# A graph network's node update: one product moved to the dealing stage, and the edge counts laid on all partitions

## The chip, the cores and the metric

The kernel runs on one core of one Trainium2 chip. The metric is device time in microseconds, the median over the timed runs. A profiled execution, which is a run of its own, gives the trace. Engines: PE (TensorE), DVE (VectorE), ACT (ScalarE), POOL (GpSimd), SP (SyncE, which only issues transfers here).

## The reference, cut to what matters

Four layers follow one another over a graph of 3125 nodes (256 features each) and 53125 edges: a message-passing layer, a mixture of experts, a mean-aggregation layer and an MLP over chosen tokens. The change touches the first:

```python
msg_input  = concatenate([node[i], node[j], edge_attr])        # 256 + 256 + 16
h          = relu(msg_input @ mW1 + mb1)                       # 512 hidden units, per edge
messages   = h @ mW2 + mb2                                     # 256
aggregated = segment_sum(messages, i)                          # over the edges of node i
u          = relu(concatenate([node, aggregated]) @ uW1 + ub1) # 512
x          = node + u @ uW2 + ub2
```

`node` is the layer-normalized input. The sum over edges is linear, so the kernel sums `h` per node first and multiplies by `mW2` once per node; `mb2` then comes in times the number of the node's edges, `deg`. All is float32 at the ends; some products work with rounded halves.

## The kernel before, in words

The nodes lie in 25 blocks of 128 (`NB`), the edges in 416 tiles of 128, taken as 104 chunks of four tiles.

**Dealing** (`deal`). The loop over chunks `c` sorts the edges into buckets of 32 source nodes. For each chunk, `buckets` makes one-hots on DVE, `select` ranks the edges by products on PE, `place` works out each edge's row on DVE and builds the edge's record `rt` (with a copy by ACT), and `put` has POOL store the four tiles with one indirect transfer each into `cbuf`. `rt` and its row number `to` have rings of 20 buffers. For the first 13 chunks, `halve_attributes` also turns the edge attributes on PE. The order on PE, DVE, ACT and SP is the one written; POOL runs free and works off its stores.

Into the same loop is woven the generator `tables`, which goes through the 25 node blocks. For each block it normalizes the rows (DVE), turns them (PE, L133, into `xTa`), makes the two node products of the message layer (`pp`, L314 and L316), copies and splits them (ACT, DVE) and stores five tiles through SP: `tab_b`, `tab_a`, two halves in `tab_h`, and the turned rows in `xT0`. It yields four times a block, and the loop takes one step from it in each chunk from `c >= 3` on: 101 steps for 100 yields. At `c == 2` the loop splits the attribute weights `w_ea` (L420, L421), which SP has loaded after the first eight node blocks and `mw1`. After the loop, a check of the counts writes `fits`, on which all engines branch.

**Buckets** (`edges_by_bucket`). 125 steps: 25 units of four buckets, five rounds each. A step makes the source side by PE (`spread`, `pa`), adds the gathered target side `cb` on DVE, takes the relu on ACT (`relu`), and sums the hidden units by source on PE (`by_source`, `ph`). POOL gathers `cb` from `tab_b` three steps ahead (L712). Two generators fill the gaps: `tally` (`counts`: one-hots `oa`, `ob` on DVE, products `pn` on PE, copies `cn` on ACT, stored by SP) and `nodes_left` (`finish_nodes` for the last pair of node blocks: `update`, normalization, `experts`, normalization, `sends`). A step takes up to four slots of the first and three of the second. At the end of a unit `close` copies the summed hidden units into `hsb` and puts the edge counts into its last column.

`update` works on a pair of blocks. It loads the pair's turned rows (`xT0g`), turns the sums (L529) and the counts (`pdeg`, L532, one row), multiplies by `mW2` with the counts times `mb2` as a last product over one partition (`pagg`, L539, L541), copies to `aT` (L542), makes four output groups of `uW1` with `dense` (L514 on PE: two products with `xT0g`, two with `aT`; then relu with bias on ACT, L515), and multiplies by `uW2` (`pupd`, L554, added to `x` on DVE at L556). Three PSUM banks are shared in turn by all small products of this stage.

After the buckets come the mean-aggregation layer (`sums_of_few`, `padj`) and the MLP, which the change does not touch.

Of the kernel before, what the change touches and what calls it, by code (L numbers as in the profile page):

```python
# [11 lines left out]
I32 = mybir.dt.int32  # L12
# [38 lines left out]
def gnn_ffn_kernel(ctx: ExitStack, tc: tile.TileContext, a: dict, out: bass.AP):  # L51
# [103 lines left out]
    xT0 = dram.tile([P, 2, NP], F32, name="xT0")  # L155
# [21 lines left out]
    def deal():  # L177
# [46 lines left out]
        for k in range(0, NB - 1, 8):  # L224
            nc.sync.dma_start(x[:, k:k + 8, :], a["x"][k * P:(k + 8) * P].rearrange("(k p) d -> p k d", p=P))
            if k == 0:
# [5 lines left out]
                nc.vector.memset(one_row, 1.0)  # L232
                w_ea = tp.tile([32, HID], F32, name="w_ea", bufs=1)
# [69 lines left out]
        def tables():  # L303
            for k in range(NB):
                xns = layernorm_rows(k, 1, True, nc.vector)
                yield
                xT = tp.tile([P, 2, P], F32, name="xTa")
# [22 lines left out]
                nc.sync.dma_start(xT0[:, :, rows], xT)  # L330
# [3 lines left out]
        with tc.tile_pool(name="deal", bufs=3) as dp:  # L334
# [34 lines left out]
            def place(c, out):  # L369
# [10 lines left out]
                to, f = dp.tile([P, GB], I32, name="to", bufs=20), dp.tile([P, GB], F32, name="f")  # L380
# [5 lines left out]
                rt = dp.tile([P, GB, RW], F32, name="rt", bufs=20)  # L386
# [19 lines left out]
            for c in range(-1, chunks):  # L406
# [17 lines left out]
                if c >= 3:  # L424
                    next(making, None)
# [35 lines left out]
    def rest_of(fast):  # L461
# [17 lines left out]
        mb2 = load(wl0, "mb2", [1, D], a["L0_gnn_mb2"].rearrange("(o m) -> o m", o=1))  # L479
        uw1 = weight(wl0, "uw1", a["L0_gnn_uW1"])  # L480
        ub1 = col_bias(wl0, "ub1", a["L0_gnn_ub1"], HID)
# [37 lines left out]
        def update(k0, nb, sums):  # L519
            n = nb * P  # L520
            xT = st["up"].tile([P, 2, UB * P], F32, name="xT0g")
            nc.sync.dma_start(xT[:, :, :n], xT0[:, :, k0 * P:k0 * P + n])
            hT = st["up"].tile([P, 4, UB * P], F32, name="hT", bufs=1)
            deg = st["up"].tile([1, UB * P], F32, name="deg", bufs=1)
            for i in range(nb):
                h0 = sums[i]
# [4 lines left out]
                pg = bank("pdeg")  # L531
                nc.tensor.matmul(pg[:1, :P], lhsT=h0[:, HID:HW], rhs=ident, start=True, stop=True)  # L532
                nc.vector.tensor_copy(deg[:, i * P:(i + 1) * P], pg[:1, :P])
                yield
            aT = st["up"].tile([P, 2, UB * P], F32, name="aT", bufs=1)
            for m in range(2):
                pd = bank("pagg")
                for c in range(4):
                    nc.tensor.matmul(pd[:, :n], lhsT=mw2[:, c, m * P:(m + 1) * P], rhs=hT[:, c, :n],  # L539
                                     start=c == 0, stop=False)  # L540
                nc.tensor.matmul(pd[:, :n], lhsT=mb2[:, m * P:(m + 1) * P], rhs=deg[:, :n], start=False, stop=True)  # L541
                nc.vector.tensor_copy(aT[:, m, :n], pd[:, :n])  # L542
                yield
            uT = st["up"].tile([P, 4, UB * P], F32, name="uT", bufs=1)
            ins = [xT[:, c, :n] for c in range(2)] + [aT[:, c, :n] for c in range(2)]
            for m in range(4):
                dense(uT[:, m, :n], [uw1[:, c, m * P:(m + 1) * P] for c in range(4)], ins, n, ub1[:, m:m + 1])
# [836 lines left out]
```

## Time and profile before

| | |
|---|---|
| median of 3 timed runs | 2482.83 us (2481.05 to 2484.32) |
| profiled execution | 2345.68 us, of which span 2343.4 us |
| mean granted PE clock in it | 0.863 |
| busy: PE, DVE, ACT, POOL | 1863.8, 1452.8, 952.0, 985.8 us |
| POOL's stores of dealt edges (L396) | 416, 992 ns each |
| POOL's gathers (L712) | 490, 978 ns each |
| `pp` on PE while edges are dealt (L314) | 200, 852 ns each |
| transfers, over the span | 309.76 MB, mean 132 GB/s |

A row of a window or of a group gives an engine's busy time in it, and the number of its instructions in parentheses. PE's matmuls are pipelined and overlap in the records, so a row of eight that spans 1.7 us costs 0.22 us each, whatever the mean of one says. A line of the waits reads: engine and line that waited, `<-` what ended the wait, the total in us, how often, and the longest.

### The profile page before, as it was taken

The numbers are of one execution on the slowest core, as the hardware profiler recorded it, in microseconds if no ns is written. First come the engines' busy times: TensorE is split into PE (matmuls) and PEld (weight loads), VectorE is DVE, ScalarE is ACT, GpSimd is POOL, SyncE is SP. The second block draws the span as 40 slices with busy tenths as digits, with TensorE's granted clock in tenths as the row PEclk, the third lists the DMA queues.
The fourth block names the chain that finished last, engine by engine and source line by source line (L and its number), as shares of the span: only waits on it lengthen the run. The fifth ranks groups of instructions, "written<-read, shape, count | busy, mean of one in ns | idle before, by whom it ended". The sixth has DMA issues, their size and how long they took to land. (4 is left out here: it accounts for less than half of the span.)

```text
span 2343.4 us, 26626 instructions
## 1 busy us (share of the span) xinstructions
PE 1863.8 (80%) x8262; PEld 1121.3 (48%) x8262; DVE 1452.8 (62%) x3985; ACT 952.0 (41%) x1682; POOL 985.8 (42%) x1032
## 2 busy tenths in 40 slices
PE   3787787820488988888988988988868999998598
PEld 1333333310154554554554544544535777885366
DVE  5777777730376666666666666666536765668921
ACT  1222222200366655655655655655423333442111
POOL 3777777776564544544554554454100000110000
PEclk9767676755698988998998998999978999999799
DMA  9223223221975655655655655664125456540010
GB/s 276 88 88 104 91 91 105 88 68 45 304 226 151 194 160 153 199 175 149 196 176 155 190 174 163 185 174 135 48 79 158 114 130 157 127 112 1 0 37 21
DMA packets 234590, 309.76 MB, mean 132 GB/s; under 512 B 34313, under 2 KB 165236, under 8 KB 234070
## 3 DMA queue, kind: packets, MB, share of 16 engines
q1 hardware_dynamic: 178358, 157.62, 22.7%
q0 software_dynamic: 52512, 142.96, 21.1%
q10 hardware_dynamic: 3568, 7.38, 0.9%
q8 instruction: 68, 1.11, 0.2%
q14 instruction: 84, 0.69, 0.1%
HBM read 226.18 MB, written 81.69 MB: 131 GB/s over the span
## 5 line engine op out<-in xcount | busy, mean ns | idle before, releaser
L712 POOL DMA_INDIRECT cb<-tab_b,goes_to x490 | 479.4, 978 | 533.7 <-issue 239.6
L396 POOL DMA_INDIRECT cbuf<-rt,to x416 | 412.6, 992 | 162.9 <-issue 99.3
L750 DVE TENSOR_TENSOR cb<-pa,cb 128x1024 f32<-128x1024 f32 x245 | 288.8, 1217 | 181.5 <-PE pa L745 152.2
L1279 PE MATMUL padj<-z,slab 128*128 128x512 f32 x1250 | 320.0, 409 | 15.7 <-DVE z L1188 15.4
L755 ACT ACTIVATE cb<-cb 128x1024 f32<-128x1024 f32 x245 | 257.7, 1052 | 101.8 <-DVE cb L750 98.7
L1279 PEld LDWEIGHTS padj<-z,slab 128*128 128x128 f32 x1250 | 232.3, 191 | 74.7 <-issue 24.0
L745 PE MATMUL pa<-gives,oT 128*128 128x512 f32 x490 | 175.6, 486 | 36.2 <-ACT oT L107 31.6
L107 ACT ACTIVATE oT<-pt 64x512 fp32r<-64x512 f32 (+1 forms) x250 | 144.5, 578 | 132.9 <-PE pt L731 129.1
L802 PE MATMUL pn<-ob,oa 128*128 128x448 f16 (+1 forms) x692 | 160.5, 351 | 21.1 <-DVE ob L787 8.3
L125 POOL TENSOR_TENSOR x<-x,xn 128x256 f32<-128x256 f32 x25 | 24.5, 978 | 351.5 <-DVE xn L122 351.5
L783 DVE TENSOR_SCALAR oa<-ids,rows 128x128 f16<-128x128 f16 x692 | 163.1, 262 | 0.0
L787 DVE TENSOR_SCALAR ob<-ids,rows 128x448 f16<-128x448 f16 (+1 forms) x490 | 161.6, 330 | 0.0
L133 PE MATMUL pt<-ident,xn 128*128 128x128 f32 x200 | 52.5, 361 | 128.1 <-DVE xn L122 64.3
L314 PE MATMUL pp<-mw,xTa 128*128 128x512 f32 x200 | 142.7, 852 | 0.0
L761 PE MATMUL ph<-cb,rows 128*32 128x512 f32 x980 | 140.4, 623 | 0.0
L745 PEld LDWEIGHTS pa<-gives,oT 128*128 128x128 f32 x490 | 102.6, 221 | 69.5 <-ACT oT L107 43.5
L107 ACT ACTIVATE cn<-pn 128x352 f16<-128x352 f32 x196 | 98.0, 500 | 93.2 <-PE pn L802 74.1
L731 PE MATMUL pt<-ident_r,rows 128*64 128x128 f32 x490 | 56.8, 238 | 91.1 <-DVE goes_to L705 91.1
L731 PEld LDWEIGHTS pt<-ident_r,rows 128*64 128x64 f32 x490 | 39.7, 139 | 178.6 <-issue 139.5
L514 PE MATMUL pd<-xT,fw 128*128 128x512 f32 (+1 forms) x224 | 92.7, 570 | 34.2 <-DVE y L1330 34.2
L1206 ACT ACTIVATE slab<-two 128x2048 fp32r<-128x2048 f16 x50 | 95.6, 1911 | 41.1 <-PE padj L1279 38.8
L117 ACT ACTIVATE rstd<-mv,eps 128x1 f32<-128x1 f32 (+1 forms) x76 | 22.4, 295 | 220.7 <-DVE mv L115 220.7
(224 smaller groups left out, 3163.7 us busy)
## 6 DMA issues: line engine op xcount, KB each, us to landing
two<-adj_h SPq DMA_DIRECT2D x24, 1600.0 KB, 8.1
rows<-cbuf SPq DMA_DIRECT2D x25, 680.0 KB, 8.5
gives<-tab_h SPq DMA_DIRECT2D x48, 256.0 KB, 8.8
adj_h<-cn SPq DMA_DIRECT2D x100, 112.0 KB, 2.5
adj_h<-cn SPq DMA_DIRECT2D x100, 88.0 KB, 3.2
cb<-tab_b,goes_to POOLq DMA_INDIRECT x490, 4.1
cbuf<-rt,to POOLq DMA_INDIRECT x416, 2.2
cbuf<-empty ACTq DMA_DIRECT2D x4, 1632.0 KB
```

The lines of the kernel that those rows point to most:

```text
L107: nc.scalar.activation(dst, src, AF.Copy)
L314: nc.tensor.matmul(pp, lhsT=xT[:, c, :], rhs=mw1[:, 2 * h + c, :], start=c == 0, stop=h == 1 and c == 1)
L396: one_of = nc.gpsimd.indirect_dma_start(out=cbuf[:], out_offset=bass.IndirectOffsetOnAxis(ap=to[:n, i:i + 1], axis=0), in_=rt[:n, i, :], i ...
L712: nc.gpsimd.indirect_dma_start(out=cb[:, j, :], out_offset=None, in_=tab_b[:], in_offset=bass.IndirectOffsetOnAxis(ap=u["to"][:, i:i + 1], ...
L745: nc.tensor.matmul(got[j // 2][:, j % 2, :], lhsT=oT[:, j, :], rhs=u["ag"][:, j, :], start=True, stop=True)
L750: nc.vector.tensor_tensor(cb[:, j:j + 2], pa, cb[:, j:j + 2], op=OP.add)
L755: nc.scalar.activation(h, h, AF.Relu)
L761: nc.tensor.matmul(u["ph"][j * BN:(j + 1) * BN, :], lhsT=u["rows"][:, GB * r + j, :BN].bitcast(F32), rhs=hs[j // 2][:, j % 2, :], start=r ...
L783: nc.vector.tensor_scalar(oa, ids[:, 1 + i * P:1 + (i + 1) * P], field[:, 0:1], None, op0=OP.is_equal)
L787: nc.vector.tensor_scalar(ob[:, :w], ids[:, 1:w + 1], field[:, 1:2], None, op0=OP.is_equal)
L802: nc.tensor.matmul(pn[:, :w], lhsT=u["oa"].pop((j, r, i)), rhs=u["ob"][j, r][:, :w], start=r == rs[0], stop=r == rs[-1])
L1279: nc.tensor.matmul(pa, lhsT=slab[:, c, :], rhs=(z2 if second else z1)[:, c, :], start=c == 0, stop=c == NB - 1)
```

## The change

The product of the normalized rows with the upper half of `uW1` moves from `update` into `tables`. `tables` now keeps the turned rows of two blocks in one tile; after the second it makes four groups of 128 outputs (two products each, over 256 columns), ACT adds the bias `ub1` and writes `ut`, and one store puts it in `own` (DRAM, 512 outputs by node), in place of the stores of `xT0`. `uw1a` and `ub1` are therefore loaded in `deal`, ahead of `w_ea`. `tables` yields 14 times a pair, 177 times in all, and the loop takes one step in even chunks and two in odd ones. The rings of `rt` and `to` go from 20 to 12.

`update` loads `ux` from `own` instead of `xT0g`; it makes only the two products with `aT`, adds `ux` on DVE, and takes the relu on ACT for two groups at a time. The edge counts come from `close` on all 128 partitions (the one-hot sums multiplied by ones), so the turns of `pdeg` and the one-partition products go, and `aT` is made by one DVE operation for each block: counts times `mb2`, now a value per partition, plus `pd`. The path through `hsum` (`deg is None`), which runs only if the edges don't fit, makes the counts in `update`.

```diff
--- before.py
+++ after.py
@@ -152,7 +152,7 @@
     zres = dram.tile([NP, 2 * D], F32, name="zres")
 
 
-    xT0 = dram.tile([P, 2, NP], F32, name="xT0")
+    own = dram.tile([P, 4, NP], F32, name="own")
 
     first = ExitStack()
     ring(first)
@@ -230,6 +230,9 @@
                 nc.sync.dma_start(mb1, a["L0_gnn_mb1"].rearrange("(o m) -> o m", o=1))
                 one_row = tp.tile([1, P], F32, name="one_row", bufs=1)
                 nc.vector.memset(one_row, 1.0)
+                uw1a = tp.tile([P, 2, HID], F32, name="uw1a", bufs=1)
+                nc.sync.dma_start(uw1a, a["L0_gnn_uW1"][:D].rearrange("(k p) m -> p k m", p=P))
+                ub1 = col_bias(tp, "ub1", a["L0_gnn_ub1"], HID)
                 w_ea = tp.tile([32, HID], F32, name="w_ea", bufs=1)
                 for i in range(2):
                     nc.sync.dma_start(w_ea[16 * i:16 * (i + 1)], a["L0_gnn_mW1"][2 * D:2 * D + 16])
@@ -301,10 +304,14 @@
 
 
         def tables():
+            pair = []
             for k in range(NB):
                 xns = layernorm_rows(k, 1, True, nc.vector)
                 yield
-                xT = tp.tile([P, 2, P], F32, name="xTa")
+                if not pair:
+                    two = tp.tile([P, 2, UB * P], F32, name="xTa")
+                pair.append(two)
+                xT = two[:, :, (len(pair) - 1) * P:len(pair) * P]
                 layernorm_turn(xns, xT)
                 yield
                 ts = []
@@ -327,7 +334,19 @@
                 nc.sync.dma_start(tab_a[rows, :], ts[0])
                 nc.sync.dma_start(tab_h[rows, 0, :], first.bitcast(F32))
                 nc.sync.dma_start(tab_h[rows, 1, :], rest.bitcast(F32))
-                nc.sync.dma_start(xT0[:, :, rows], xT)
+                yield
+                if k % UB == UB - 1 or k == NB - 1:
+                    n = len(pair) * P
+                    ut = tp.tile([P, 4, UB * P], F32, name="ut", bufs=1)
+                    for m in range(4):
+                        pu = bank("pu")
+                        for c in range(2):
+                            nc.tensor.matmul(pu[:, :n], lhsT=uw1a[:, c, m * P:(m + 1) * P], rhs=pair[0][:, c, :n],
+                                             start=c == 0, stop=c == 1)
+                        nc.scalar.activation(ut[:, m, :n], pu[:, :n], AF.Identity, bias=ub1[:, m:m + 1])
+                        yield
+                    nc.sync.dma_start(own[:, :, (k + 1) * P - n:(k + 1) * P], ut[:, :, :n])
+                    pair.clear()
                 yield
 
 
@@ -377,13 +396,13 @@
                 rnd = dp.tile([P, GB], I32, name="rnd")
                 nc.vector.tensor_scalar(rnd, rank, P.bit_length() - 1, None, op0=OP.logical_shift_right)
 
-                to, f = dp.tile([P, GB], I32, name="to", bufs=20), dp.tile([P, GB], F32, name="f")
+                to, f = dp.tile([P, GB], I32, name="to", bufs=12), dp.tile([P, GB], F32, name="f")
                 nc.vector.scalar_tensor_tensor(f, rnd, float(GB - P * PER), base[:, at], op0=OP.mult, op1=OP.add)
                 nc.vector.scalar_tensor_tensor(f, rank, float(PER), f, op0=OP.mult, op1=OP.add)
                 nc.vector.scalar_tensor_tensor(f, rank, float(CAP), f, op0=OP.is_lt, op1=OP.mult)
                 nc.vector.tensor_tensor(to, f, past[:, at], op=OP.add)
                 pos[c] = to
-                rt = dp.tile([P, GB, RW], F32, name="rt", bufs=20)
+                rt = dp.tile([P, GB, RW], F32, name="rt", bufs=12)
                 nc.vector.tensor_tensor(rt[:, :, :BN], nodes.unsqueeze(1).to_broadcast([P, GB, BN]),
                                         row[:, at, AT_SRC - BN:AT_SRC - BN + 1].to_broadcast([P, GB, BN]), op=OP.is_equal)
                 copy(rt[:, :, BN:], row[:, at, :])
@@ -422,7 +441,8 @@
                     nc.sync.dma_start(w_h[:, 0, :], wf.bitcast(F32))
                     nc.sync.dma_start(w_h[:, 1, :], wr.bitcast(F32))
                 if c >= 3:
-                    next(making, None)
+                    for _ in range(1 + c % 2):
+                        next(making, None)
                 if c + 2 < chunks:
                     ohs.pop(c, None)
 
@@ -476,9 +496,8 @@
             queue[0] = Held
 
         mw2 = weight(wl0, "mw2", a["L0_gnn_mW2"])
-        mb2 = load(wl0, "mb2", [1, D], a["L0_gnn_mb2"].rearrange("(o m) -> o m", o=1))
-        uw1 = weight(wl0, "uw1", a["L0_gnn_uW1"])
-        ub1 = col_bias(wl0, "ub1", a["L0_gnn_ub1"], HID)
+        mb2 = col_bias(wl0, "mb2", a["L0_gnn_mb2"], D)
+        uw1 = weight(wl0, "uw1", a["L0_gnn_uW1"][D:])
         uw2 = weight(wl0, "uw2", a["L0_gnn_uW2"])
         ub2 = row_bias(wl0, "ub2", a["L0_gnn_ub2"], D)
         sw1 = weight(wl0, "sw1", a["L0_ffn_sW1"])
@@ -518,33 +537,43 @@
 
         def update(k0, nb, sums):
             n = nb * P
-            xT = st["up"].tile([P, 2, UB * P], F32, name="xT0g")
-            nc.sync.dma_start(xT[:, :, :n], xT0[:, :, k0 * P:k0 * P + n])
+            ux = st["up"].tile([P, 4, UB * P], F32, name="ux")
+            nc.sync.dma_start(ux[:, :, :n], own[:, :, k0 * P:k0 * P + n])
             hT = st["up"].tile([P, 4, UB * P], F32, name="hT", bufs=1)
-            deg = st["up"].tile([1, UB * P], F32, name="deg", bufs=1)
+            degs = []
             for i in range(nb):
-                h0 = sums[i]
+                h0, deg = sums[i]
                 pt = bank("pt4")
                 for c in range(4):
                     nc.tensor.transpose(pt[:, c * P:(c + 1) * P], h0[:, c * P:(c + 1) * P], ident)
                 copy(hT[:, :, i * P:(i + 1) * P], pt.rearrange("p (c n) -> p c n", c=4))
-                pg = bank("pdeg")
-                nc.tensor.matmul(pg[:1, :P], lhsT=h0[:, HID:HW], rhs=ident, start=True, stop=True)
-                nc.vector.tensor_copy(deg[:, i * P:(i + 1) * P], pg[:1, :P])
+                if deg is None:
+
+                    deg = st["up"].tile([P, P], F32, name="deg")
+                    pg = bank("pdeg")
+                    nc.tensor.matmul(pg[:, :P], lhsT=h0[:, HID:HW].to_broadcast([P, P]), rhs=ident, start=True, stop=True)
+                    nc.vector.tensor_copy(deg, pg[:, :P])
+                degs.append(deg)
                 yield
             aT = st["up"].tile([P, 2, UB * P], F32, name="aT", bufs=1)
             for m in range(2):
                 pd = bank("pagg")
                 for c in range(4):
                     nc.tensor.matmul(pd[:, :n], lhsT=mw2[:, c, m * P:(m + 1) * P], rhs=hT[:, c, :n],
-                                     start=c == 0, stop=False)
-                nc.tensor.matmul(pd[:, :n], lhsT=mb2[:, m * P:(m + 1) * P], rhs=deg[:, :n], start=False, stop=True)
-                nc.vector.tensor_copy(aT[:, m, :n], pd[:, :n])
+                                     start=c == 0, stop=c == 3)
+                for i in range(nb):
+                    nodes_of = slice(i * P, (i + 1) * P)
+                    nc.vector.scalar_tensor_tensor(aT[:, m, nodes_of], degs[i], mb2[:, m:m + 1], pd[:, nodes_of],
+                                                   op0=OP.mult, op1=OP.add)
                 yield
             uT = st["up"].tile([P, 4, UB * P], F32, name="uT", bufs=1)
-            ins = [xT[:, c, :n] for c in range(2)] + [aT[:, c, :n] for c in range(2)]
             for m in range(4):
-                dense(uT[:, m, :n], [uw1[:, c, m * P:(m + 1) * P] for c in range(4)], ins, n, ub1[:, m:m + 1])
+                pd = bank("pd")
+                for c in range(2):
+                    nc.tensor.matmul(pd[:, :n], lhsT=uw1[:, c, m * P:(m + 1) * P], rhs=aT[:, c, :n], start=c == 0, stop=c == 1)
+                nc.vector.tensor_tensor(uT[:, m, :n], pd[:, :n], ux[:, m, :n], op=OP.add)
+                if m % 2:
+                    nc.scalar.activation(uT[:, m - 1:m + 1, :n], uT[:, m - 1:m + 1, :n], AF.Relu)
                 yield
             for i in range(nb):
                 k = k0 + i
@@ -763,14 +792,17 @@
 
                 def close(u):
                     m = u["m"]
-                    hs = bp.tile([P, HW], F32, name="hsb", bufs=3)
-                    copy(hs[:m, :HID], u["ph"][:m])
+                    hs = bp.tile([P, HID], F32, name="hsb", bufs=3)
+                    copy(hs[:m], u["ph"][:m])
+                    deg = bp.tile([P, P], F32, name="degs", bufs=3)
                     pt = bank("pt")
-                    nc.tensor.matmul(pt[:m, :1], lhsT=u["oss"].rearrange("p j s -> p (j s)")[:, :m], rhs=one, start=True, stop=True)
-                    copy(hs[:m, HID:HW], pt[:m, :1])
+                    nc.tensor.matmul(pt[:, :m], lhsT=one.to_broadcast([P, P]), rhs=u["oss"].rearrange("p j s -> p (j s)")[:, :m],
+                                     start=True, stop=True)
+                    copy(deg[:, :m], pt[:, :m])
                     if m < P:
                         nc.vector.memset(hs[m:], 0.0)
-                    return hs
+                        nc.vector.memset(deg[:, m:], 0.0)
+                    return hs, deg
 
                 def one_hots(u, j, rs):
 
@@ -1055,7 +1087,7 @@
                     for k in range(k0, k0 + nb):
                         hs = st["up"].tile([P, HW], F32, name="h0")
                         nc.sync.dma_start(hs, hsum[k * P:(k + 1) * P, :])
-                        got.append(hs)
+                        got.append((hs, None))
                     for _ in finish_nodes((k0, nb), got):
                         pass
             rings.pop()
```

## The prediction, made before the change was run

> **What bounds the kernel now.** I read the page's slices first, then a table of windows, then the steps of one pair of node blocks, then the waits.
>
> The 40 slices show three stages: dealing the edges until slice 10, the buckets with the node update until slice 29, then the last convolution and the MLP. One wide window for each of the first two, and one for the tail of the first (columns: window, its length, busy us and count for each engine, granted clock, DMA share, GB/s):
>
> ```profile
> 60.00:480.00 420.00, 330.09 (x1286) 141.02 (x1285) 309.80 (x1026) 107.64 (x323) 319.71 (x322) 0.71 0.29 95
> 490.00:580.00 90.00, 0.19 (x2) 0.11 (x2) 3.06 (x9) 0.00 (x0) 67.50 (x71) 0.50 0.10 31
> 640.00:1640.00 1000.00, 863.53 (x4263) 515.23 (x4262) 667.24 (x1915) 595.05 (x1002) 503.02 (x532) 0.92 0.59 175
> ```
>
> From 490 to 580 us PE, DVE and ACT stand idle and POOL alone works off indirect stores: the dealing stage ends with POOL, whose last store ends at 578.8 us. Its pace is 90 us over 71 stores, 1.27 us each, 5.1 us for a chunk of four. The other engines deal 98 chunks in 420 us, 4.3 us each, so they end 90 us early. In the buckets PE is busy 86% at a clock of 0.92. What waits confirms it: SP, which would load the first bucket, sits behind those stores, and in the bucket stage others wait for PE:
>
> ```profile
> SPq L695 <- DMA cbuf<-rt,to: 85.4, 5, 80.8
> ACT uT L515 <- PE pd L514: 65.8, 33, 2.8
> DVE aT L542 <- PE pagg L541: 29.0, 11, 2.7
> PE pdeg L532 <- ACT oT L107: 14.2, 10, 1.4
> ```
>
> Then one pair of node blocks, cut at the starts of four bucket steps; `update` runs in them:
>
> ```profile
> 1026.20:1032.00 5.80, 4.39 (x33) 2.56 (x32) 4.48 (x13) 4.73 (x7) 4.51 (x5) 1.00 0.77 220
> 1032.00:1042.65 10.65, 10.40 (x53) 6.71 (x52) 7.35 (x27) 5.02 (x9) 5.13 (x7) 1.00 0.94 297
> 1042.65:1051.35 8.70, 8.70 (x49) 6.31 (x48) 5.90 (x15) 5.35 (x10) 4.60 (x6) 1.00 0.50 143
> 1051.35:1059.15 7.80, 7.80 (x45) 5.12 (x44) 4.84 (x12) 4.86 (x8) 1.98 (x3) 1.00 0.37 114
> ```
>
> PE fills the second to fourth window (10.40 of 10.65, 8.70 of 8.70, 7.80 of 7.80). The update's matmuls set these steps' length, so what is taken from PE here shortens them until DVE (7.35, 5.90) is full.
>
> **The change part by part.** Sums are against the profiled execution, 2345.68 us (span 2343.4). The median of the timed runs, 2482.83, lies 137 us or 5.8% above it; nothing here says where those are spent, so I scale the difference by 1.058.
>
> *Taken from the bucket stage, per full pair (12 of them).* The product with the nodes' own features is 16 matmul instructions. Back to back the chain has eight of `pd L514` in 1.73 us, so 0.216 each: 3.5 us. The two bias products (`pagg<-deg,mb`, L541) hold PE from 1034.86 to 1035.48: 0.62 each, 1.2 us. The two degree turns (`pdeg`, L532) take about 0.5 us, and the wait of 1.4 us before one of them may go or move to the next user of that bank; I take half, 0.7. Sum 5.9 us.
>
> *Given back per pair.* (a) Today the own-feature matmuls run while DVE copies `aT`; without them the first product waits for two 128-column scalar_tensor_tensors, about 0.3 us each (the 128-column `aT` copy took 0.29): 0.6 us. (b) The four sums with `ux` come to DVE, at the 0.42 us of L556 1.7 us, three of them in the third window. There DVE would need 5.90+1.26 = 7.2 us while PE needs 8.7-2.6 = 6.1: 1.1 us of that gain is lost. Queued behind a DVE that waits for `pd` are the one-hots of the tally and the next `cb` sum; PE uses one-hots made a slot earlier, so I charge no more. ACT does two relus of 512 columns where it did four of 256. (c) `close` now moves 128 columns instead of one, and ACT copies 128 instead of one: 0.1+0.12 us, twice: 0.4. So 5.9-0.6-1.1-0.4 = 3.8 us a pair, 46 us for 12. The single last block stands on the end's path with 128 columns (0.44 us for four matmuls, four times, and two biases): some 2 us net. **Gain 48 us.** From both sides: 24 us if all of the own-feature saving is lost on DVE, 73 us if nothing is given back.
>
> *`ux` load.* 512 KB for 256. The 256 KB load lands 5.1 us after issue, the 640 KB of `z<-zres` takes 11.0. It is issued at 1028.3 and needed near 1040.5: hidden with 1 to 7 us left. Were that cover gone, 0 to 3 us a pair. The weights held back for the second stage shrink by 512 KB beside the first gathers: 0 to 2 us of gain, taken as nothing.
>
> *Put into the dealing stage.* First, `uw1a` (512 KB) and `ub1` are queued on SP ahead of `w_ea`.
>
> ```profile
> w_ea<-in_L_gnn_mW_dram SPq DMA_DIRECT2D x2, 32.0 KB, 9.9
> ACT w_h L420 <- DMA w_ea<-in_L_gnn_mW_dram: 20.6, 1, 20.6
> ```
>
> All of ACT, DVE and PE wait for `w_ea` there (DVE 19.3 us behind ACT, PE 20.8 behind DVE), POOL's reserve runs out and it idles 4.0 us before 57.7. 512 KB at the 271 GB/s of that window is 1.9 us, the issues and the 4-byte pieces of `ub1` about 1: POOL starts its run 3 us later, and POOL is the bound, so +3. Second, chunks 3 to 13 also turn edge attributes (12 chunks in 60 us, 5.0 each) and now carry 1.5 table steps each instead of one; at about 5.5 POOL starves 0.4 over seven chunks: +3 (0 to 6).
>
> Third, the products themselves. Here a rule speaks against the change. The trace: the same line `pp` L314 takes 3.75 us for four matmuls of 512 columns at 308.4 us and 1.98 for four at 313.2, the mean granted clock is 0.71 here against 0.92 in the buckets. The Trainium skill (TensorE: Matmul & The Clock Gate, Part 1: The HAM clock gate) says the array's clock is halved until some 3.4 us of sustained activity release it. By the full-speed row a group of 16 costs 3.5 us; by the rule, each burst of four after a pause costs double, 7.5 us from the slow row. I take the middle, 5.5 a pair. The activations on ACT (52 at 0.47 us, L515: 24 us) fit beside, ACT being busy 108 of 420. ScalarE: Activation LUTs (Table sets) lists identity among the cheap functions in every set, so I charge no table load; no run here shows an Identity.
>
> The loop's pace: a block took 4 chunks, 17.1 us. Now it takes 14 steps for two blocks at 3 steps per 2 chunks, 4.67 chunks a block. That is 17.1, plus 0.67 plain chunks of 2.9 (1.9), plus half a product group (1.7 to 3.8), plus 0 to 2 where row statistics and their transposes fall in one iteration and PE waits for DVE: 20.7 to 24.8 us, 4.4 to 5.3 a chunk. I take 4.8, under POOL's 5.1. The rings of 12 chunks (61 us of POOL work) hold DVE back only if the pace is under 4.7; then POOL is never short. Loop end: 63+99x4.8 = 538 us. The generator has 177 steps, the loop takes 152; 25 are left behind it: three table blocks (about 9 us each), two and a quarter product groups, SP's table stores and the check of `fits` (6 us), about 38 us together: 576 us, against POOL's end at 579+6 = 585. Hidden, but with 9 us left where there were 86. SP has 13 `own` stores for 25 of `xT`, ahead of the load of `rows`; it sits idle for ACT most of the stage. **Cost 6 us.**
>
> Net -42 in the profiled execution: 2304; -44 on the median: **2438**.
>
> **The rivals.** *The tail comes out from under POOL (slower).* At a pace above 4.89 a chunk the 25 leftover steps end after POOL. At 5.5 (PE always at half clock and stalled) the loop ends at 607, the tail at 645 instead of 579: +67, less 48: +19, **2503**. It decides from 5.3 a chunk on, where the whole gain is eaten. For it: the clock row 0.71, and DVE's waits for `t0h` (69.9 us in this stage) show PE late. Against it: PE was busy 79%, POOL alone for 90 us. Chance 0.27.
>
> *DVE takes PE's place in the update.* ACT's 65.8 us of waits for `pd` become DVE's, with the `cb` sums behind them. The gain is then 24 at best; if half the waits delay the next `cb` sum, -24+33+6 = +15: 2467 to **2499**, most likely near 2480. For: DVE 7.35 of 10.65 and busier than ACT. Against: it idles 33% in the stage. Chance 0.15.
>
> *Nothing is given back.* -73 and 6 in dealing: -67, **2412**. Chance 0.06.
>
> **How the numbers follow.** The forecast has 0.52; its own range, gain 30 to 65 and cost 3 to 10, is 2420 to 2462. About 0.2%, 5 us, is what a measurement of this kernel can tell from no change. The forecast and the third rival are faster (0.58). Of the first rival 0.06 is faster, 0.03 the same, 0.18 slower; of the second 0.04, 0.03, 0.08. Faster 0.68, same 0.06, slower 0.26. The range reaches over most of both rivals: 2402 to 2500.
>
> **What would show it.** Right: `pd` in the buckets halves (416 matmuls to 208), the windows of the update shrink by 1.5 to 2 us each with DVE near 7 of 7, the bucket stage is some 46 us shorter, POOL's last deal store ends near 585 and SP's wait for `cbuf` at L695 falls from 80 us to about 10. Wrong: DVE, PE and SP still work on tables after POOL's last store, with the first `rows` load late by tens of us; or DVE waits for `pd` with PE idle behind it and the steps no shorter.

## Result: slower by 1.3%, and what the profile after shows

The changed kernel takes 2513.28 us (median of 4; 2507.48 to 2521.52), before 2481.94 beside it: ratio 1.0132, 95% interval 1.0107 to 1.0156. Its profiled execution took 2517.74 us. The forecast was 2438 us, with a range of 2402 to 2500.

One thing must be known to read this. The profiled execution of before that the prediction was worked from (2345.68 us) was one that did not come again: profiled once more, the same program took 2497.15 us. It was taken on a chip on which the median of before is 2497.41 us, 15.5 more than beside the changed kernel. What follows compares the changed kernel with this second profile, so the difference of the profiles below is smaller than that of the timed runs, +31.3 us, which were taken side by side. Stage ends in us, from the first load of `rows` (the dealing is over), the first load of `two` (the buckets are over) and the span:

| profile | dealing | buckets | rest | span |
|---|---|---|---|---|
| before, first | 580.0 | 1136.9 | 626.5 | 2343.4 |
| before, second | 685.7 | 1182.5 | 626.6 | 2494.8 |
| changed | 731.1 | 1162.9 | 621.4 | 2515.4 |

So the change costs 45.4 us in the dealing and wins 19.6 in the buckets and 5.2 behind them: +20.6 in these two executions. The other profiles of this case bear the gain out: with the old bucket stage the buckets take 1174 to 1188 us in them, with the whole of the new one 1159 to 1172. The loss is less certain in size: `own_only` below, which has the dealing of the changed kernel and ran on the second profile's chip, reaches the first load of `rows` at 721.5, a loss of 35.8. And the 151 us between the two profiles of before lie in the dealing (106) and the buckets (46), none in the rest.

The wide windows of the changed kernel that answer to those shown of before, and the 46 us between its last dealt chunk and the first load of `rows`:

```profile
60.00:480.00 420.00, 255.77 (x983) 121.51 (x984) 209.94 (x689) 82.80 (x241) 260.36 (x268) 0.69 0.20 67
490.00:580.00 90.00, 55.92 (x216) 27.25 (x215) 44.21 (x147) 17.11 (x50) 55.19 (x58) 0.70 0.20 69
685.00:731.00 46.00, 36.45 (x95) 18.31 (x92) 13.38 (x42) 12.62 (x30) 6.61 (x7) 0.76 0.36 126
860.00:1860.00 1000.00, 830.13 (x3896) 487.31 (x3893) 671.84 (x1915) 570.20 (x959) 461.47 (x499) 0.88 0.56 166
```

The stretch from 490 to 580, POOL's alone in the first profile, is ordinary dealing here. In the third line PE is busy 36.5 of 46 us and POOL has 7 stores left: most of the leftover table steps stand in the open. The same windows of the second profile of before (its buckets lie 80 us earlier):

```profile
60.00:480.00 420.00, 254.78 (x906) 105.98 (x905) 215.77 (x716) 75.72 (x224) 260.96 (x269) 0.63 0.21 71
490.00:580.00 90.00, 51.24 (x183) 20.78 (x181) 42.53 (x140) 15.56 (x46) 53.14 (x55) 0.62 0.22 74
780.00:1780.00 1000.00, 851.61 (x4140) 512.55 (x4134) 641.68 (x1841) 575.25 (x966) 476.23 (x507) 0.90 0.58 167
```

POOL issues 269 stores in 420 us instead of 322, and PE and ACT go on until 668: POOL works on behind them for 16 us, not for 90. The wait that stood for POOL as the bound, SP's 85.4 us for `cbuf`, is gone from before itself. From the waits of the second profile, SP's line and those of the dealing, 60 to 686 us (us in total, times, longest):

```profile
SPq L695 <- DMA cbuf<-rt,to: 0.9, 1, 0.9
...
POOL cbuf L396 <- issue: 163.7, 341, 7.3
DVE own L373 <- remote: 159.9, 21, 9.5
PE pk L354 <- ACT total L107: 158.9, 23, 8.8
ACT total L107 <- remote: 143.3, 24, 8.7
```

"remote" means that nothing recorded ended when the wait did. DVE waits there for `pk` and ACT for `ptot`, both products of PE, which by PE's own records were done some 4 to 9 us before; PE then waits for ACT's `total`, and POOL gets its records from the other three. About once a table block PE, DVE and ACT stand idle together: between 60 and 660 us the trace has 21 such stretches of over 2 us, the longest 7.2, and 113 us in all, which is the size of the 106 us. The first profile has no such wait and no such stretch at all.

One more mark tells the two profiles apart. Both hold the same 26626 instructions. But of the 8513 semaphore steps with which PE, DVE and ACT report a finished instruction, the first trace holds 8497 and the second 6854. The missing ones lie in the dealing and the buckets, where the two executions differ in time too, and none behind them. Every other profile of this case lacks 17 to 22% of these steps. The timed executions have a granted clock on record as well, so none of them is known to have run unrecorded. Whether the recording itself holds the engines up, or only suffers from the same cause, no run here tests.

### The profile page after: what moved, and what is told of

Read it like the earlier page. It is cut to its first block, busy times and chain, and to the rows that moved or that the text cites. A ratio compares the mean times of both kernels' runs of the same rounds, so it can differ in the third digit from the quotient of the medians.

```text
span 2515.4 us, 26538 instructions
## 1 busy us (share of the span) xinstructions
PE 1918.5 (76%) x8160; PEld 1144.3 (45%) x8160; DVE 1482.8 (59%) x4037; ACT 967.9 (38%) x1708; POOL 969.0 (39%) x1032
## 5 line engine op out<-in xcount | busy, mean ns | idle before, releaser
L741 POOL DMA_INDIRECT cb<-tab_b,goes_to x490 | 469.8, 959 | 600.9 <-issue 279.1
L415 POOL DMA_INDIRECT cbuf<-rt,to x416 | 405.5, 975 | 287.9 <-issue 182.4
L774 PE MATMUL pa<-gives,oT 128*128 128x512 f32 x490 | 187.9, 515 | 37.2 <-ACT oT L107 32.3
L834 PE MATMUL pn<-ob,oa 128*128 128x448 f16 (+1 forms) x692 | 168.6, 358 | 43.3 <-issue 11.5
L321 PE MATMUL pp<-mw,xTa 128*128 128x512 f32 x200 | 156.6, 928 | 39.4 <-ACT xTa L107 36.5
L815 DVE TENSOR_SCALAR oa<-ids,rows 128x128 f16<-128x128 f16 x692 | 168.3, 270 | 0.0
L774 PEld LDWEIGHTS pa<-gives,oT 128*128 128x128 f32 x490 | 109.6, 237 | 77.2 <-ACT oT L107 44.1
L392 DVE TENSOR_TENSOR own<-pk,oh 128x392 f32<-128x392 f32 x104 | 58.4, 561 | 143.1 <-remote 77.6
L373 PE MATMUL pk<-total,ones 1*128 1x392 f16 x103 | 41.8, 406 | 122.5 <-ACT total L107 91.3
L107 ACT ACTIVATE total<-ptot 1x98 f16<-1x98 f32 x103 | 24.7, 240 | 265.8 <-remote 202.8
```

Source lines behind the costliest of these rows:

```text
L107: nc.scalar.activation(dst, src, AF.Copy)
L321: nc.tensor.matmul(pp, lhsT=xT[:, c, :], rhs=mw1[:, 2 * h + c, :], start=c == 0, stop=h == 1 and c == 1)
L415: one_of = nc.gpsimd.indirect_dma_start(out=cbuf[:], out_offset=bass.IndirectOffsetOnAxis(ap=to[:n, i:i + 1], axis=0), in_=rt[:n, i, :], i ...
L741: nc.gpsimd.indirect_dma_start(out=cb[:, j, :], out_offset=None, in_=tab_b[:], in_offset=bass.IndirectOffsetOnAxis(ap=u["to"][:, i:i + 1], ...
L774: nc.tensor.matmul(got[j // 2][:, j % 2, :], lhsT=oT[:, j, :], rhs=u["ag"][:, j, :], start=True, stop=True)
L815: nc.vector.tensor_scalar(oa, ids[:, 1 + i * P:1 + (i + 1) * P], field[:, 0:1], None, op0=OP.is_equal)
```

## The experiments

Ratios are against before on the same chip, whose median was 2482 to 2507 us; stage ends are from one profile of each, and two profiles of the same dealing (the changed kernel's 731.1 and `own_only`'s 721.5) lie 9.6 us apart.

**The kernel before, profiled once more** (no edit).

> The kernel before, unchanged, profiled once more. Its profiled execution took 2345.68 us, its timed runs 2482, and nothing said where the 137 us lie. Theory S (the stalls that the profile of the changed kernel shows in the dealing, in which PE, DVE and ACT stand idle together for 2 to 7 us, are in the usual run of the kernel before too): a profile near 2482 with such stalls, POOL's last deal store near 690 rather than 579, the bucket stage as long as before. Theory L (the change itself brings the stalls): POOL's last store near 580 again, and any difference spread evenly over all stages as the granted clock is.

Measured: 2497.15 us; first `rows` load at 685.7, POOL's last store at 683.6, ACT's late wait for `ptot` 24 times. Theory S holds for the dealing; the bucket stage, expected as before, is 46 us longer too, most of it in one step of each pair (4.83 us in the first profile, 7.57 here).

**Shorter rings.** `bufs=20` of `to` and `rt` to 12.

> The kernel before with the rings of `to` and `rt` at 12 in place of 20, nothing else. Theory R (12 chunks are too few: DVE and ACT wait for POOL's stores, and POOL then for them): slower by 20 us or more, with DVE's and ACT's waits for the rings in the dealing. Theory P (the pace of the dealing is set by the steps of the tables and POOL alone): within 5 us of before.

Measured: ratio 0.9989 (0.9975 to 1.0002), first `rows` load at 684.4. Theory R falls: the shorter rings of the change cost nothing there.

**Each half of the change alone.** `counts_only` is before with the new `close`, `deg` and `aT`; `own_only` is the changed kernel with the old ones.

Cut and shortened:

```
# counts_only, in update
-    matmul(pd, lhsT=mb2[:, m], rhs=deg)          # before: on PE
+    scalar_tensor_tensor(aT[:, m, nodes_of], degs[i], mb2[:, m:m + 1], pd[:, nodes_of], mult, add)
```

> The kernel before with the edge counts alone put on all partitions (close, deg, the two scalar_tensor_tensors for aT), the product with the own features left whole in the update, nothing changed in the dealing. By the prediction's terms: two bias products 1.2, two degree turns 0.5, a wait 0.7, less the longer copies 0.4 and the aT wait 0.3 (hidden behind own-feature matmuls here): 2 us a pair, 25 us in all: 2457. Theory V (DVE is the bound of the update's steps): no gain, within 5 us of 2482.

> The changed kernel with the edge counts as before (a bias product on PE, the count of a block on one partition), so only the product with the own features is moved. Theory T (the moved product delays the dealing by more than it saves): slower than before by 30 to 60 us, and than the changed kernel by 10 to 25. Theory V (the counts are what costs, on DVE): faster than the changed kernel.

Measured: `counts_only` 1.0021 (1.0006 to 1.0036), `own_only` 1.0146 (1.0114 to 1.0178). The first `rows` load is at 686.1 with the counts alone and at 721.5 with the moved product alone. So the loss is the moved product's (theory T), and it lies in the dealing; the further 10 to 25 us that T gave `own_only` over the changed kernel did not come (1.0146 beside 1.0132). The counts win 6 us of the bucket stage in the profile and nothing in the timed runs, as theory V had it in number.

**Where in the dealing: the products or the steps.** `empty_steps` leaves the `pu` products and their activations out, so that `own` holds zeros, and keeps every step and store (lines shortened).

```
-    for c in range(2): nc.tensor.matmul(pu[:, :n], lhsT=uw1a[...], rhs=pair[0][...])
-    nc.scalar.activation(ut[:, m, :n], pu[:, :n], AF.Identity, bias=ub1[:, m:m + 1])
+    if k == UB - 1: nc.vector.memset(ut[:, m, :], 0.0)
     yield
```

> The changed kernel with the 104 `pu` matmuls and their 52 activations left out of the dealing (`own` is stored from zeros); steps, pace and stores stay. Theory W (the products' work on PE and ACT costs): first `rows` load near 690, POOL's last store near 685, time some 35 us under the changed kernel, near 2495 on the chip where before takes 2497. Theory N (the steps' number and pace cost): first `rows` load still between 715 and 731, time within 10 us of the changed kernel.

Measured, in one execution: 2515.13 us where before takes 2499.80 (1.006), first `rows` load at 727.5, against 731.1 with the products. Theory W falls: without the products the dealing is still 41.8 us longer than before's, so most of the cost is the steps'. What the 13 groups of products cost is less sure: 3.6 us in the profiles, less than the 9.6 between two profiles of one dealing, and some 18 by the ratios (1.006 for 1.0132).

**The leftover steps.** `two_steps`: two steps a chunk; `even`: 1.8, so that they end with the loop; `before_two`: the kernel before with two.

```
-    for _ in range(1 + c % 2):
+    for _ in range(2):                                # two_steps
+    for _ in range(9 * (c + 1) // 5 - 9 * c // 5):    # even
         next(making, None)
```

> The changed kernel with two table steps in each chunk from the fourth on, in place of 1.5, so that all 177 fit in the loop and none is left behind it. In its profile the loop ended at 685 and the leftover steps held the first load of `rows` until 731. Theory N (the tail of 25 steps is the cost: a chain in which each engine waits for the others): first `rows` load at 700 or earlier, 25 us or more faster than the changed kernel, near 2487. Theory W (the work that was put into the dealing is what costs, wherever it stands): the loop grows by what the tail loses, first `rows` load between 720 and 731, within 8 us of the changed kernel.

> The kernel before with two table steps in each chunk from the fourth on, in place of one, so that the tables are done half way through the dealing. It is the control for the changed kernel with two steps (2480 where before took 2500). Theory M (the change itself, at a pace that hides its steps, is worth the 16 to 20 us of the bucket stage): no gain here, 2490 to 2508, first `rows` load near 686. Theory P (the gain came from the pace alone): 2465 to 2485, first `rows` load at 670 or earlier.

> The changed kernel with 1.8 table steps a chunk (nine in five chunks), so that the 177 steps end with the loop: neither a tail of 25 steps (first `rows` load at 731) nor tables that are done 15 chunks early (two a chunk, 683). Theory N (what stands behind the loop is what costs, the rest is carried by the pace): first `rows` load at 665 to 683, time 0.990 to 0.994 of before, 40 us or more under the changed kernel's ratio. Theory Q (the steps of two a chunk gain because the last 15 chunks run free of table work): first `rows` load at 690 to 715, time 0.995 to 1.005 of before.

Measured: `two_steps` 0.9935 (0.9907 to 0.9962), `even` 1.0006 (0.9981 to 1.0031), `before_two` 1.0160 (1.0131 to 1.0189). The last products of the loop and the first loads of `rows`, from the views of these tiles; times are ns (min/median/max) and then first and last start in us. Before, second profile:

```profile
L354 PE MATMUL pk<-total,ones x103: 334/502/504, 20.0 to 667.9; 1*128 1x392 f16 x103
...
L695 SPq DMA_DIRECT2D rows<-cbuf x25: 102/374/571, 685.7 to 1744.4; - x25
```

The changed kernel:

```profile
L373 PE MATMUL pk<-total,ones x103: 321/335/504, 20.0 to 685.2; 1*128 1x392 f16 x103
...
L724 SPq DMA_DIRECT2D rows<-cbuf x25: 3/373/1442, 731.1 to 1770.9; - x25
```

Two steps a chunk:

```profile
L373 PE MATMUL pk<-total,ones x103: 321/335/504, 20.0 to 666.9; 1*128 1x392 f16 x103
...
L724 SPq DMA_DIRECT2D rows<-cbuf x25: 3/387/671, 683.0 to 1724.1; - x25
```

1.8 steps a chunk:

```profile
L373 PE MATMUL pk<-total,ones x103: 321/335/504, 20.1 to 680.3; 1*128 1x392 f16 x103
...
L724 SPq DMA_DIRECT2D rows<-cbuf x25: 282/475/1673, 702.8 to 1751.4; - x25
```

From the last product to the first load it is 17.8 us in before, 45.9 in the changed kernel, 16.1 and 22.5 with two and 1.8 steps. So the 25 leftover steps are most of what the change lost: 28 of its 45.4 us stand behind the loop and 17 in a longer loop (32 and 4 of 35.8 in `own_only`), and with all the same work in the loop the first `rows` load comes 28 to 48 us earlier. `even` came out by theory Q's numbers, not N's: some 20 us of what two steps gain are not the tail. That they come from the chunks without table steps at the end (12 by the count of 177 steps from chunk 3 on, not 15) is not shown: on the kernel before, two steps leave some 50 such chunks and cost 1.6% (first `rows` load at 710.9), which neither of its theories allowed for.

**What makes the pace 6.1 to 6.3 us a chunk.** Five kernels look for the cause of the late results. The edits: `split_pp` has a `yield` between the two halves of a block's table products; `spread_stores` issues a block's stores over four steps; `thin_pp` keeps two of a block's four products and leaves out the others and the bias, so its tables are incomplete; `warm_before` and `poke_before` add products into an unread bank behind `ptot`:

```
+    for i in range(8):        # warm_before: 392 columns each
+        nc.tensor.matmul(warm[:, :GB * NBK], lhsT=later, rhs=oh, start=i == 0, stop=i == 7)
+    for i in range(8):        # poke_before: one column each, and once a block behind pp
+        nc.tensor.matmul(none[:1, :1], lhsT=ones[:, :1], rhs=ones[:, :1], start=i == 0, stop=i == 7)
```

> The kernel before with the table products `pp` of a block in two steps, one half a chunk, in place of both in one; the number of steps is the same. In a usual run of the kernel before the dealing has one stall of 4 to 7 us per table block (24 of them, DVE's and ACT's waits for PE add up to some 150 us each), right behind the eight fp32 products and beside the 1.25 MB of table stores. Theory F (the long fp32 run on PE brings the stall): most of the stalls go, first load of `rows` 50 to 100 us earlier than 686, time 2400 to 2445. Theory D (the burst of stores brings it): stalls as before, within 10 us of 2497.

> The kernel before with a block's table stores issued one or two a step over four steps (`tab_b` and `xT0` at once, then `tab_a`, then the two halves of `tab_h`), in place of all five together. Theory D (the burst of 1.25 MB holds up PE's results): the stalls shrink to a third, first load of `rows` 60 to 100 us earlier than 686, time 2400 to 2440. Theory F (the fp32 run on PE does it): stalls as before, within 10 us of 2497.

> The kernel before with two of a block's four pairs of table products and the bias products left out: two fp32 products of 512 columns a block where there were eight records and two (the tables hold a part of the sums). Theory F (the long fp32 run on PE brings the stalls of 4 to 7 us behind it): stalls of over 2 us gone, first `rows` load at 600 or earlier, where POOL's 5.1 us a chunk ends the dealing. Theory L (PE's results come late for another reason, and the fp32 run only stands beside it): stalls of the same length at every block, first `rows` load at 640 or later.

> The kernel before with eight more f16 matmuls of 392 columns a chunk in the dealing, into a bank that nothing reads (some 1.3 us of PE at the full clock, 2.6 at half). In the usual run PE's results reach DVE and ACT 5 to 17 us after PE's own records, at a granted clock of 0.5 to 0.63 and with PE idle about 40% of the time. Theory C (the array is gated down because it idles; work keeps it up): granted clock above 0.75, stalls gone, first `rows` load at 600 to 645, time 2400 to 2455. Theory H (PE's load is what holds it up): the pace gets worse by 1 to 2.6 us a chunk, first `rows` load at 720 or later, 2530 or more.

> The kernel before with eight one-column f16 matmuls into an unread bank right behind the counts (`ptot`) of each chunk, and eight behind a block's table products: some 0.5 us of PE a chunk and hardly any work. In the kernel with eight long matmuls at that place ACT's late waits for `ptot` fell from 143 us to 33, while those for the table products rose to 229. Theory G (a result is reported late when nothing follows it on PE, and whatever follows pushes it out): the late waits of ACT and DVE in the dealing fall below 60 us together, where the usual run of before has 300, first `rows` load at 640 or earlier, time under 0.975 of before. Theory K (not what follows, but the amount of work moved those waits): late waits as before, first `rows` load at 686 or later, 0.998 to 1.02 of before.

| kernel | ratio (interval) | first `rows` load |
|---|---|---|
| `split_pp` | 0.9936 (0.9916 to 0.9956) | 669.0 |
| `spread_stores` | 0.9997 (0.9982 to 1.0011) | 689.2 |
| `thin_pp` | one time: 2472.96 beside 2506.66 | 656.6 |
| `warm_before` | 1.0254 (1.0220 to 1.0288) | 747.0 |
| `poke_before` | 1.0242 (1.0203 to 1.0281) | 739.2 |

`split_pp` came out between its theories: 17 us earlier, but with most of the late waits still there. The stores are not it (theory D falls). With four fp32 records a block in place of ten the late waits do not go; the two below grow to 393 us together, from the 303 of before shown above. The waits of `thin_pp` from 60 to 660 us:

```profile
ACT total L107 <- remote: 261.0, 31, 12.4
...
DVE own L370 <- remote: 131.6, 17, 10.8
```

So theory L: the first `rows` load came only 29 us earlier, and the late results stayed. Theory C of `warm_before` falls too, theory H's numbers came, and here the clock and the time part. Two windows of `warm_before`; the same two of before, second profile, have a granted clock of 0.64 and 0.64:

```profile
60.00:180.00 120.00, 86.55 (x404) 42.12 (x402) 60.27 (x195) 24.39 (x68) 72.18 (x74) 0.81 0.18 62
180.00:300.00 120.00, 78.23 (x372) 36.49 (x372) 56.56 (x191) 17.53 (x58) 64.98 (x68) 0.78 0.20 69
```

The Trainium skill (TensorE: Matmul & The Clock Gate, Part 1: The HAM clock gate) has sustained activity lift the array's clock; the column before the last two agrees (0.81 and 0.78 for 0.64), and the dealing was 61 us longer all the same. Eight one-column products cost nearly as much as eight of 392 columns (+53 us for some 990, +61 for some 790), so it is not the number of columns that costs. Both moved the late waits from `ptot` to the table products. The waits of `warm_before` from 60 to 740 us:

```profile
ACT t L107 <- remote: 229.0, 25, 12.9
...
ACT total L107 <- remote: 32.9, 7, 5.4
```

Theory G falls: `poke_before` lost even a little more than theory K allowed, though G's picture (what follows a result pushes it out) fits where the waits went. The cause stays open.

**A version that beats both.** `two_split` is two steps a chunk and split table products; `even_split` the same with 1.8; `warm_two` and `poke_two` add the unread products.

> The changed kernel with two steps a chunk, and the table products of a block in two steps (which took 16 us from the kernel before). If the length of the fp32 run on PE costs by itself, the two add up: near 2464, first `rows` load near 667. If both only move the same waits, no more than 5 us under the 2480 of two steps alone.

> The same 1.8 steps a chunk, with a block's table products in two steps besides. Theory N: first `rows` load at 660 to 680, time 0.986 to 0.991 of before, the shortest of all. Theory Q: as with two steps and split, 0.991, or longer.

> The changed kernel with two steps a chunk and the same eight unread f16 matmuls a chunk. Theory C (idling gates the array): first `rows` load at 600 to 650 where it was 683, time 2390 to 2445. Theory H (load): first `rows` load at 715 or later, 2510 or more.

> The changed kernel with two steps a chunk and split table products (0.991 of before), with the same one-column matmuls. Theory G: first `rows` load at 640 or earlier where it was 680, 0.975 of before or less. Theory K: 0.99 to 1.01 of before.

Measured: `two_split` 0.9913 (0.9895 to 0.9932), first `rows` load at 680.5; `even_split` 0.9920 (0.9894 to 0.9946), at 697.3, by theory Q again; `warm_two` 1.0149 (1.0088 to 1.0209), at 716.7; `poke_two` 1.0091 (1.0060 to 1.0123), at 735.3. Theories C and G fall here too. Splitting adds little to two steps, and `two_split` has the lowest ratio, 0.9% under before and some 2% under the changed kernel; from `even_split` its interval does not part it. Whether the change is worth anything on top of `split_pp` alone (0.9936) these intervals do not tell.

## Why the prediction was wrong, point by point

**The cover (the step that failed).** "576 us, against POOL's end at 579+6 = 585. Hidden" rests on 90 us in which POOL works alone. They belonged to that one execution: in the second profile of before it is 16. The prediction saw that its profile lay 137 us under the median, and wrote "nothing here says where those are spent, so I scale the difference by 1.058". Spread evenly, they would leave the cover in place; in truth 106 us lie in the dealing and eat it. In a usual run the loop ends at 667.9 and POOL's last store starts at 683.6: POOL waits for the other engines, not they for POOL. So the tail had nothing to hide under, and the dealing cost 45.4 us (35.8 in `own_only`) where the sum had 6; with a gain of 24.8 for 48, -42 became +20.6.

**The pace and the tail.** The pace was forecast at 4.4 to 5.3 us a chunk and is 6.3 ((685.2-62)/99), but before has 6.1 already. The tail came near its forecast: about 38 us, where the prediction's own terms add up to 45 (27 for three blocks, 12.4 for the product groups at 5.5, 6 for the check), and 45.9 measured, 11 of them under POOL's stores. The first rival, "the tail comes out from under POOL", is what happened, by a slower loop in both kernels rather than by the moved products. It was priced at 67 less 48, +19; measured are 45 less 25, +21. That the two sums agree is luck: both terms are off by some 22 us. And its point of decision, 5.3 us a chunk, had been passed before the change was made.

**The products' clock.** The prediction weighed 3.5 us a group against 7.5 and took 5.5. The question had little weight: all 13 groups cost 3.6 us in the dealing by the profiles, some 18 by the ratios. The activations with Identity brought no table load: ACT has 29 before and after. `w_ea` came later by about what was forecast (3 us): ACT starts on it at 53.7, in the two profiles of before at 52.3 and 51.4.

**The gain in the buckets.** Forecast 48 (46, and 2 for the last block, behind them), measured 24.8 (19.6 and 5.2). `pd` has 208 records where it had 416:

```profile
L573 PE MATMUL pd<-aT,uw x208: 275/379/796, 840.4 to 1895.6; 128*128 128x256 f32 x96, 128*128 128x128 f32 x8
```

Four of a pair's ten bucket steps, each from the start of its second `cb` sum to the first of the next step (the two sums of a step start 1.14 us apart), us, medians over ten pairs, and the mean length of a pair:

| step | before, first | before, second | `counts_only` | `own_only` | changed |
|---|---|---|---|---|---|
| 2nd: `hT`, `pagg` | 4.83 | 7.57 | 7.42 | 7.58 | 7.35 |
| 3rd: `aT`, two `pd` | 8.47 | 8.48 | 6.99 | 7.77 | 6.75 |
| 4th: two `pd` | 7.56 | 7.56 | 7.57 | 6.81 | 7.25 |
| 9th: `pex`, `psh` | 10.47 | 10.44 | 11.54 | 12.16 | 12.07 |
| pair | 89.0 | 92.4 | 91.7 | 92.1 | 90.8 |

Alone, each half does what its terms said: the moved product takes 0.71 and 0.75 off the third and fourth step, 1.5 us for 1.8 forecast (3.5-0.6-1.1), the counts 1.5 to 1.6 for 2.0. Together they do not add up: 1.73 for 2.20 in the third step and 0.31 for 0.74 in the fourth, where DVE is the fuller engine. The third and fourth step of one pair, before (second profile):

```profile
1256.90:1266.52 9.62, 7.97 (x42) 4.93 (x41) 5.54 (x17) 4.94 (x8) 3.70 (x4) 1.00 0.67 178
1266.52:1275.23 8.71, 8.71 (x48) 6.32 (x47) 5.91 (x16) 5.36 (x10) 4.60 (x6) 1.00 0.50 143
```

and after:

```profile
1294.85:1302.65 7.80, 6.33 (x35) 3.89 (x35) 6.27 (x20) 4.07 (x6) 2.00 (x3) 1.00 0.72 207
1302.65:1311.06 8.41, 6.73 (x36) 3.88 (x35) 7.66 (x19) 3.79 (x7) 6.86 (x8) 1.00 0.70 190
```

In the fourth, DVE goes from 5.91 to 7.66 us and PE from 8.71 to 6.73: the work left PE and 0.3 us left the step. That is the term of 1.1 us for a full DVE, which was too small here, and a part of the second rival. The waits say the same; ACT waits for DVE here where it waited for PE's `pd` (79.6 us in the second profile of before):

```profile
ACT uT L576 <- DVE uT L574: 50.3, 14, 4.6
```

The rest was given back where no term looked: the ninth step is longer by 1.1 to 1.7 us in the median (0.4 to 0.7 in the mean) in all three kernels, which neither the update nor `close` touches, and the third has a pause of 1.5 to 2.6 us in five of eleven pairs of the changed kernel. Why is not shown.

**The signs named.** "DVE, PE and SP still work on tables after POOL's last store, first `rows` load late by tens of us" came true: SP's last store of `own` starts at 728.7, 33 us after POOL's last. The windows shrank by 1.7 and 0.3 us, not by 1.5 to 2 each. (The lower end of the forecast's own range, 2420, is 2417 by its terms; nothing hangs on it.)

## What to carry to other kernels

A profiled execution that lies 6% under the median is not a scaled copy of the usual one. Before building on an idle stretch in it, profile again; a cover of 90 us that only one execution shows is no cover. Work that is given out in steps beside a loop can hide inside the loop but not behind it: here the moved work cost the dealing nothing at two steps a chunk, 17 us at 1.8, and 36 to 45 with 25 steps left over. Count the steps against the loop's iterations first, and set the pace so that none is left; then measure the pace itself, for the same two steps a chunk cost the kernel before 1.6%.

## What the runs showed of the hardware

PE's records can be far ahead of what other engines see. The timeline of `two_steps`, after its last table step and with PE nearly idle (busy 2.1 us from 645 to 665; start us, duration, engine and line, then the idle time before it):

```profile
646.65 0.48 PE L373 MATMUL pk<-total,ones 1*128 1x392 f16 x1 [5.14 <-ACT total L107]
...
647.47 0.24 PE L378 MATMUL ptot<-total,ones 1*1 1x98 f16 x1
...
654.77 0.57 DVE L392 TENSOR_TENSOR own<-pk,oh 128x392 f32<-128x392 f32 x1 [9.89 <-remote]
...
664.63 0.24 ACT L107 ACTIVATE total<-ptot 1x98 f16<-1x98 f32 x1 [17.79 <-remote]
664.82 0.32 ACT L107 ACTIVATE rt<-row 128x144 f32<-128x144 f32 x1
664.93 0.48 PE L373 MATMUL pk<-total,ones 1*128 1x392 f16 x1 [16.29 <-ACT total L107]
665.44 0.57 DVE L392 TENSOR_TENSOR own<-pk,oh 128x392 f32<-128x392 f32 x1 [7.82 <-PE pk L373]
```

DVE takes up `pk` 7.6 us after PE's record ends, ACT takes up `ptot` 16.9 us after its own; 18 us later the pair of PE and DVE needs 0.03. It is PE's report that is late, not the engine that waits: in the trace PE's semaphore steps at 654.75, 0.02 us before DVE starts, and next at 664.55 and 664.61, the last 0.02 us before ACT starts. The load on PE does not explain it (next to none here), nor does the granted clock alone (0.50 in the late and the prompt stretch), nor the stores of the tables (none any more). In the kernel before, one execution had none of it in the dealing and took 6% less; its trace is also the only one with nearly all semaphore steps. Which of PE's array, its signals, the chip's state or the recording is behind it, these runs leave open.
